# Layer 1 of a four-layer graph network: one joined float32r product for two weights of the turned h, and a new order of the steps around it

## The chip, the cores and the metric

The kernel runs on one core of a Trainium2 chip. The metric is the device time of one execution in microseconds, the median of several runs.

The engines are named as in the profile: PE multiplies matrices, PEld is its loading of the stationary operand, DVE, ACT and POOL work on elements, and SP issues the transfers (DMAs). Each engine takes its instructions in the order in which they were queued.

## What is computed

There are 32 graphs (batches) with the same 512 nodes and 128 features each, one 512x512 matrix `adj`, and four layers. Every layer is `x = x + layer(relu(layernorm(x)))`. Layer 1, the one that the change is in, is in the reference

```python
def _cheb_hops(x0, A, orders):
    x1 = jnp.einsum('bnf,nw->bwf', x0, A)
    ...
    x2 = 2.0 * jnp.einsum('bnf,nw->bwf', x1, A) - x0
...
xs = [X] + _cheb_hops(X, A1, 2) + _cheb_hops(X, A2, 2)
out = jax.nn.relu(stack(xs) @ Theta1 + bias)
```

with A1 and A2 both equal to `adj`. Since both hop lists are the same, the kernel adds up the five 128x128 blocks of Theta1 to three weights and computes, for h the normalised x,

- x1 = adj^T h,
- w = h th1 + x1 th2,
- x = x + relu(h th0 + adj^T w + b1).

Layer 0 is a masked attention with fixed scores, layer 2 a message layer with the squares of `adj` as its weights, and layer 3 an attention.

## The kernel before

**Names.** Two batches make a pair q (16 pairs). Two pairs make a round r of layer 1 (8 rounds), A = 2r and C = 2r + 1. Node blocks of 128 are counted by t or i (NT = 4). A product "of 512 columns" streams 512 columns of the moving operand past a 128x128 stationary one.

**Three parts.** Where a product must be nearly as exact as float32 but cheaper, both operands are split into three float32r tiles, `high`, `low` and `mid`, and the three products are added up in one PSUM bank. `moving_parts` (L420 to L422) makes them of an SBUF tile with one operation each on ACT, POOL and DVE; `bank_parts` does the like for a PSUM bank with one on ACT and two on DVE. The constants UP and DOWN belong to this splitting.

**The steps of layer 1**, all in `layer1` (L950 on):

- `normalised(q)`: h of a pair, eight ACT operations (L285), from statistics that DVE and ACT made before (`stats_steps`, L239 on).
- `turn(q)`: h is turned feature-major: DVE transposes 32x32 blocks, SP writes them to DRAM in four transfers (L328) and reads them back in one (L330). `straighten(q)` has POOL copy the result into `hs[q]` in plain order (L974).
- `split_up(q, b)`: the three parts of h of one batch.
- `first(q, b)`: x1 of one batch, turned, from the parts of h and of adj: twelve float32r products of 512 columns (L405), and one ACT copy out of PSUM (L407).
- `weighed(q, b)`: w of one batch: for each t two float32 products of 128 columns, `hs` with `th[:, 1]` and x1 with `th[:, 2]` (L447, through `projected`), and three operations that split the bank into the parts of w (L992 to L994).
- `mix(r, i)`: the output of one node block for the four batches of a round: four float32 products `hs` with `th[:, 0]` (L999), twelve float32r products of 512 columns, adj parts with w parts (L1003), then two DVE operations, one with the bias and one for relu and residual (L1005, L1007).

In the profile a float32 product is two instructions, a float32r product is one.

**What sets the order.** The kernel is laid out by hand: on PE, DVE, ACT and POOL the order of the calls in the source is the order of the queue. In round r the mixes of round r - 1 come first, then `first(A,1)`, the two `weighed` of A, the two `first` of C, the two `weighed` of C, and `first` of the next A. For layer 1's own turns the SP queue is ordered by the program builder; for the transfers of layer 2 and of the square it is the source order.

**Buffers.** `small_tile` has 13 buffers of 512 columns (parts of h, x1), `wide_tile` six of four times that (parts of w, the parts of the squared adj), the tag `hT` four (turned h before and after straightening), PSUM eight banks.

**What runs beside.** `square` (L1337 on) is a generator that loads `adj` in a crossed order, squares it and splits it into parts on POOL for layer 2; `go(square, n)` takes n steps of it. In the kernel before the load is in round 3 and the POOL steps lie in rounds 4 to 6. `ln_stats` makes the statistics of finished pairs for layer 2, one round after their mix. `more(step)` is the entry of layer 2: normalising, turning and fetching its first batches in the last round, and its first two `features`. `late_parts` makes the three weights `th` and the parts of adj, late in layer 0.

Of the kernel before, what the change touches and what calls it, by code (L numbers as in the profile page):

```python
# [9 lines left out]
F32 = mybir.dt.float32  # L10
# [19 lines left out]
def kernel(  # L30
# [369 lines left out]
    def mixed_parts(name, left, right, dst):  # L400

        p = bank(f"p_{name}")
        for part in range(3):
            for t in range(NT):
                nc.tensor.matmul(p, right[part][:, blk(t)], left[part][:, t, :],  # L405
                                 start=(t == 0 and part == 0), stop=(t == NT - 1 and part == 2))
        nc.scalar.activation(dst, p, AF.Copy, scale=UP)  # L407

    def three(name):
        return [small_tile(f"{part}_{name}", F32R) for part in PARTS]  # L410
# [7 lines left out]
    def moving_parts(x, high, low, mid):  # L418

        nc.scalar.activation(high, x, AF.Copy, scale=DOWN)  # L420
        nc.gpsimd.tensor_sub(low, x, high.bitcast(F32))  # L421
        nc.vector.scalar_tensor_tensor(mid, x, 1.0 / UP, high.bitcast(F32), OP.mult, OP.subtract)  # L422

    def scaled_parts(x_low, high, low, mid):

# [307 lines left out]
    def late_parts():  # L733

        adj_parts.extend(matrix_tile(f"adj_{part}", F32R) for part in PARTS[:2])
        high, low = adj_parts
        for t in range(NT):
            nc.scalar.activation(high[:, t, :], adj_s[:, t, :], AF.Copy, scale=DOWN)
            tc.keep_in_program_order(nc.gpsimd.tensor_sub(adj_s[:, t, :], adj_s[:, t, :], high[:, t, :].bitcast(F32)))
            yield  # L740
        for out, op, p, q in ((1, OP.add, 1, 3), (2, OP.add, 2, 4), (0, OP.subtract, 0, 2)):
            tc.keep_in_program_order(nc.gpsimd.tensor_tensor(th[:, out, :], th[:, p, :], th[:, q, :], op))
        tc.keep_in_program_order(nc.gpsimd.tensor_scalar(th[:, 2, :], th[:, 2, :], 2.0, None, OP.mult))
        nc.gpsimd.tensor_scalar(th[:, 0, :], th[:, 0, :], 1.0 / UP, None, OP.mult)
# [205 lines left out]
    def layer1(more, square):  # L950


        h, hT, hs, parts, x1, w = {}, {}, {}, {}, {}, {}
        normal, turning = {}, {}

        def normalised(q, n=2 * NT):
# [19 lines left out]
        def split_up(q, b):  # L976
            if q < NQ:
                parts[q, b] = three(f"h_{q}_{b}")
                moving_parts(h[q][:, b].rearrange("p t f -> p (t f)"), *parts[q, b])

        def first(q, b):
            if q < NQ:
                x1[q, b] = small_tile(f"x1T_{q}_{b}")
                mixed_parts(f"x1T_{q}_{b}", adj_parts, parts[q, b], x1[q, b])

        def weighed(q, b):
            r, j = q // 2, 2 * (q % 2) + b
            if j == 0:
                w[r] = [wide_tile(f"w_{part}_{r}", F32R) for part in PARTS]
            p = projected(f"p_w_{q}_{b}", (columns(hs[q][:, b]), th[:, 1, :]), (columns(x1[q, b]), th[:, 2, :]))  # L990
            high, low, mid = (part.rearrange("p t (w f) -> p t w f", f=D)[:, :, j, :] for part in w[r])
            nc.scalar.activation(high, p, AF.Copy, scale=DOWN)  # L992
            nc.vector.tensor_sub(low, p, high.bitcast(F32))
            nc.vector.scalar_tensor_tensor(mid, p, 1.0 / UP, high.bitcast(F32), OP.mult, OP.subtract)  # L994

        def mix(r, i):
            p = bank(f"p_l1_{r}_{i}")
            for j in range(4):
                nc.tensor.matmul(p[:, blk(j)], columns(hs[2 * r + j // 2][:, j % 2])(i), th[:, 0, :],  # L999
                                 start=(j == 0), stop=False, skip_group_check=True)  # L1000
            for part in range(3):
                for t in range(NT):
                    nc.tensor.matmul(p, adj_parts[part][:, t, blk(i)], w[r][part][:, t, :],  # L1003
                                     start=False, stop=(part == 2 and t == NT - 1), skip_group_check=True)
            nc.vector.scalar_tensor_tensor(tiles(p), tiles(p), UP, spread(b1, 4), OP.mult, OP.add)  # L1005
            x = xq[r].rearrange("p w b t f -> p (w b) t f")[:, :, i, :]
            nc.vector.scalar_tensor_tensor(x, tiles(p), 0.0, x, OP.max, OP.add)  # L1007

# [2 lines left out]
        turn(0)  # L1011
        normalised(1)
        yield
        split_up(0, 0)
        split_up(0, 1)
        first(0, 0)
        straighten(0)
        turn(1)
        for r in range(NQ // 2):
            A, C = 2 * r, 2 * r + 1  # L1020
            last = r == NQ // 2 - 1
            if r == 0:
                first(A, 1)
                split_up(C, 0)
                split_up(C, 1)
                straighten(C)
            else:
# [8 lines left out]
                mix(r - 1, 2)  # L1036
                split_up(C, 0)
                go(square, r > 3)
                mix(r - 1, 3)
                split_up(C, 1)  # L1040
                first(A, 1)
            weighed(A, 0)
            weighed(A, 1)
            if last:
                more(0)
            go(square, r > 2)
            first(C, 0)
            normalised(A + 2, NT)
            if last:
                more(1)  # L1050
            if r:
                ln_stats(A - 2)
            else:
                go(own[NQ - 3])
                go(own[NQ - 2])
            first(C, 1)
            if last:
                more(2)
            if r:
                straighten(C)  # L1060
            split_up(A + 2, 0)
            normalised(A + 2)
            go(square, r > 3)
            weighed(C, 0)
            weighed(C, 1)
            ln_stats(C - 2) if r else go(own[NQ - 1])
            go(square, r > 3)
            turn(A + 2)
            first(A + 2, 0)
            if r == 0:  # L1070
                normalised(C + 2, 0)
        more(3)
        for i in range(NT):
            mix(r, i)
# [179 lines left out]
    def layers_2_and_3():  # L1254
# [15 lines left out]
        for n in range(B):  # L1270
# [16 lines left out]
                fetch(2, 2)  # L1287
            elif n % 2 and n + 5 < B:
                fetch(2, n // 2 + 3)
            if n in (2, 3):  # L1290
                ln_stats(NQ - 4 + n)
            if n == 12:
                weights_of_3()
            if n == 20:
# [42 lines left out]
    def square():  # L1337

        raw = wide_tile("adj_crossed")
        load_crossed(raw, adj)  # L1340
        yield
        sq.extend(wide_tile(f"sq_{part}", F32R) for part in PARTS[:2])
        for i in range(NT):
            row, (high, low) = raw[:, i, :], (part[:, i, :] for part in sq)
            nc.gpsimd.tensor_mul(row, row, row)
            nc.gpsimd.tensor_scalar(split(high), crossed(row), DOWN, 1.0, OP.mult, OP.mult)
            yield
            nc.gpsimd.tensor_sub(crossed(row), crossed(row), split(high.bitcast(F32)))
            nc.gpsimd.tensor_scalar(split(low), crossed(row), LOW, 1.0, OP.mult, OP.mult)
            yield  # L1350
        sq.append(wide_tile(f"sq_{PARTS[2]}", F32R))
        for i in range(NT):
            high, low = (part[:, i, :].bitcast(F32) for part in sq[:2])
            nc.gpsimd.tensor_sub(sq[2][:, i, :], high, low)

    made_square = square()

    def more(step):

        if step == 0:  # L1360
            chunk(2, 0)
        elif step == 1:
            chunk(2, 1)
            turn_half(2, 0)
        elif step == 2:
            turn_half(2, 1)
        elif step == 3:
            fetch(2, 0)
            chunk(2, 2)
        elif step == 4:  # L1370
            turn_half(2, 2)
            chunk(2, 3)
        elif step == 5:
            turn_half(2, 3)
            features(0)
            chunk(2, 4)
        elif step == 6:
            fetch(2, 1)
# [51 lines left out]
```

## Time and profile before

| | us |
|---|---|
| median of 3 runs (912.77 to 913.18) | 912.8 |
| the profiled execution, its own time | 912.96 |
| its span, first to last instruction | 911.2 |
| PE busy in the span | 901.1 |
| layer 1's first product to layer 2's first message product, start to start | 183.6 to 450.6 |

The profile is one execution. A row of a timeline gives the start in us from the span's beginning, the length of the merged row in us, engine, line, operation, the tiles it writes and reads, the shape and the number of instructions. A row of a table of windows gives the stretch, its length, and for PE, PEld, DVE, ACT and POOL the busy us with the number of instructions, then the granted PE clock, the share of the DMA engines and GB/s. A row of waits gives who waited for whom, the us in total, how often, and the longest. Matmuls are pipelined: what one costs in a stream is read between starts, not from its own duration.

### The profile page before, as it was taken

The numbers are of one execution on the slowest core, as the hardware profiler recorded it, in microseconds if no ns is written. First come the engines' busy times: TensorE is split into PE (matmuls) and PEld (weight loads), VectorE is DVE, ScalarE is ACT, GpSimd is POOL, SyncE is SP. The second block draws the span as 40 slices with busy tenths as digits, with TensorE's granted clock in tenths as the row PEclk, the third lists the DMA queues.
The fourth block names the chain that finished last, engine by engine and source line by source line (L and its number), as shares of the span: only waits on it lengthen the run. The fifth ranks groups of instructions, "written<-read, shape, count | busy, mean of one in ns | idle before, by whom it ended". The sixth has DMA issues, their size and how long they took to land.

```text
span 911.2 us, 15170 instructions
## 1 busy us (share of the span) xinstructions
PE 901.1 (99%) x5432; PEld 774.2 (85%) x5433; DVE 669.7 (74%) x1348; ACT 527.5 (58%) x1156; POOL 485.6 (53%) x435
## 2 busy tenths in 40 slices
PE   8999999999999999999999999999999999999998
PEld 4899999988888888888877777777789999999998
DVE  7888886566656665665767777777698888987775
ACT  5874554343532442452556768876577767666663
POOL 5867999932132163342254445545475555666553
PEclk9999999999999999999999999999999999999999
DMA  9255644123114313212332344455212223222111
GB/s 265 50 167 165 186 122 118 24 71 93 35 59 119 87 31 90 71 46 76 106 120 70 93 126 129 132 147 160 70 48 82 81 82 91 73 70 81 59 36 47
DMA packets 83915, 86.06 MB, mean 94 GB/s; under 512 B 6784, under 2 KB 74624, under 8 KB 83840
## 3 DMA queue, kind: packets, MB, share of 16 engines
q1 hardware_dynamic: 83552, 84.57, 32.8%
q8 instruction: 43, 0.70, 0.3%
q10 hardware_dynamic: 288, 0.52, 0.2%
q14 instruction: 32, 0.26, 0.1%
HBM read 44.17 MB, written 40.89 MB: 93 GB/s over the span
## 4 chain that ended last, share of the span: by engine, by line
PE 92%; ACT 3%; DVE 3%; POOL 1%; issue 0%; DMA 0%; DVEq 0%; POOLq 0%; ACTq 0%
PE p_av L1234 12%; PE p_l L1003 10%; PE p_x1T L405 9%; PE p_score L1212 9%; PE p_msgT L1142 9%; PE p_w L447 6%; PE p_l_c L393 4%; PE p_l L999 3%; PE p_l_a L393 3%; PE p_l_d L393 3%; PE p_g L447 3%; PE p_l L447 3%; PE p_hv L447 3%; PE p_feat L447 3%; PE p_phi L1151 3%; PE p_phi L1152 3%
## 5 line engine op out<-in xcount | busy, mean ns | idle before, releaser
L1234 PEld LDWEIGHTS p_av<-hv,ex 128*128 128x128 f32 x1024 | 119.3, 191 | 3.7 <-POOL ex L1207 1.0
L1234 PE MATMUL p_av<-hv,ex 128*128 128x129 f32 x1024 | 119.8, 274 | 0.8 <-POOL ex L1207 0.8
L421 POOL TENSOR_TENSOR low_feat<-feat,high_feat 128x512 fp32r<-128x512 f32 x32 | 53.9, 1686 | 115.8 <-ACT high_feat L420 111.7
L285 ACT ACTIVATE h<-x,sh,rs 128x128 f32<-128x128 f32 x256 | 102.8, 483 | 11.8 <-DVE sh L257 11.0
L1207 DVE TENSOR_TENSOR ex<-ex,adjTx 128x512 f32<-128x512 f32 x64 | 80.4, 1259 | 35.7 <-ACT ex L1205 34.0
L1207 POOL TENSOR_TENSOR ex<-ex,adjTx 128x512 f32<-128x512 f32 x64 | 98.1, 1551 | 12.2 <-ACT ex L1205 8.1
L1093 ACT ACTIVATE h<-x,sh,rs 128x128 f32<-128x128 f32 x256 | 102.9, 485 | 0.0
L428 POOL TENSOR_TENSOR key<-key 128x512 fp32r<-128x512 f32 x32 | 50.2, 1567 | 97.9 <-DVE key L427 39.8
L421 POOL TENSOR_TENSOR low_h<-h,high_h 128x512 fp32r<-128x512 f32 x32 | 47.1, 1482 | 76.6 <-ACT high_h L420 76.4
L245 DVE BATCH_NORM_STATS2 bn<-x 128x6 f32<-128x256 f32 x244 | 85.9, 417 | 0.0
L407 ACT ACTIVATE x1T<-p_x1T 128x512 f32<-128x512 f32 x32 | 19.0, 594 | 109.4 <-PE p_x1T L405 100.8
L1205 ACT ACTIVATE ex<-ex 128x512 f32<-128x512 f32 x128 | 78.9, 651 | 0.0
L1213 ACT ACTIVATE ex<-p_score 128x512 f32<-128x512 f32 x128 | 74.0, 604 | 1.4 <-PE p_score L1212 1.1
L974 POOL COPY hs<-hT 128x512 f32<-128x512 f32 x32 | 18.6, 612 | 81.5 <-DMA hT<-d_hT 81.3
L432 ACT ACTIVATE high_query<-p_query 128x512 fp32r<-128x512 f32 x32 | 19.2, 599 | 73.8 <-PE p_query L1185 73.8
L422 DVE SCALAR_TENSOR_TENSOR mid_feat<-feat,high_feat 128x512 fp32r<-128x512 f32 x32 | 28.9, 904 | 44.3 <-ACT high_feat L420 44.3
L1212 PE MATMUL p_score<-high_query,key 128*128 128x512 f32 x128 | 50.5, 394 | 0.0
L1212 PE MATMUL p_score<-low_query,key 128*128 128x512 f32 x128 | 50.3, 393 | 0.0
L1212 PE MATMUL p_score<-mid_query,key 128*128 128x512 f32 x128 | 50.3, 393 | 0.0
L447 PE MATMUL p_w<-th,x1T 128*128 128x128 f32 x256 | 49.6, 275 | 0.3 <-ACT x1T L407 0.3
L254 ACT ACTIVATE sd<-bn,eps 128x8 f32<-128x8 f32 x46 | 13.9, 302 | 61.5 <-DVE bn L245 57.4
L447 PE MATMUL p_w<-th,hs 128*128 128x128 f32 x256 | 49.4, 275 | 0.0
(220 smaller groups left out, 2350.4 us busy)
## 6 DMA issues: line engine op xcount, KB each, us to landing
d<-hb SPq DMA_DIRECT2D x128, 128.0 KB, 2.5
hT<-d SPq DMA_DIRECT2D x32, 512.0 KB, 3.4
d_hT<-hb_hT SPq DMA_DIRECT2D x112, 128.0 KB, 2.4
hT<-d_hT SPq DMA_DIRECT2D x28, 512.0 KB, 3.3
x<-in_x_dram SPq DMA_DIRECT2D x32, 256.0 KB, 5.0
out_dram<-x SPq DMA_DIRECT2D x31, 256.0 KB, 2.3
adjT_d<-adj_squares SPq DMA_DIRECT2D x4, 256.0 KB
adj_crossed<-in_adj_dram SPq DMA_DIRECT2D x4, 256.0 KB
```

Of the source, the lines that this page charges most:

```text
L245: nc.vector.bn_stats(st[:, k].rearrange("p e s -> p (e s)"), xt[q][:, b, t : t + 2, :].rearrange("p t f -> p f t"))
L285: nc.scalar.activation(h[:, b, t, :], xt[q][:, b, t, :], AF.Relu, bias=shift[q][:, i : i + 1], scale=scale[q][:, i : i + 1])
L393: nc.tensor.matmul(p[:, i * 2 * D : (i + 1) * 2 * D], a[:, k, blk(i)], b[:, k], start=(first and i == 0 and k == 0), stop=(k == 1), skip_g ...
L405: nc.tensor.matmul(p, right[part][:, blk(t)], left[part][:, t, :], start=(t == 0 and part == 0), stop=(t == NT - 1 and part == 2))
L421: nc.gpsimd.tensor_sub(low, x, high.bitcast(F32))
L447: nc.tensor.matmul(p[:, blk(t)], hT(t), w, start=(i == 0), stop=(i == len(terms) - 1))
L1003: nc.tensor.matmul(p, adj_parts[part][:, t, blk(i)], w[r][part][:, t, :], start=False, stop=(part == 2 and t == NT - 1), skip_group_check= ...
L1093: nc.scalar.activation(h[:, t, :], xt[q][:, b, t, :], AF.Relu, bias=shift[q][:, i : i + 1], scale=scale[q][:, i : i + 1])
L1142: nc.tensor.matmul(p, feats[n][part][:, blk(t)], sq[part][:, t, :], start=(t == 0 and part == 0), stop=(t == NT - 1 and part == 2))
L1207: eng.tensor_mul(split(ex[:, t, :]), split(ex[:, t, :]), crossed(mask[:, t, :]))
L1212: nc.tensor.matmul(p, keys[n][i][:, t, :], query[n][i], start=(i == 0), stop=(i == 2))
L1234: nc.tensor.matmul(po[:, i, : D + 1], ex[:, t, blk(i0 + i)], hv[:, t, :], start=(t == 0), stop=(t == NT - 1))
```

## The change

1. `weighed`: the turned h is split into three parts as well (`split_turned`: ACT, POOL, DVE), and `th[:, 0:2]`, the weights of the own term and of w, are split once (`fixed_parts`). For each t, three float32r products of 256 columns give h th0 and h th1 side by side in one half of a PSUM bank; one float32 product of 128 columns adds x1 th2 to the second half. A batch takes two banks. Each bank is read by two ACT operations (the high part of w, and the own term, which goes back into `hs`) and two DVE operations (low and mid part of w), on 128x256 elements each.
2. The own term leaves `mix`: its four float32 products go, the bias is added to the own term by POOL (`biased_own`), and the first DVE operation of the mix adds the own term in place of the bias, in two halves.
3. `square`'s load is issued in four pieces in round 1, and its POOL work, now with a pause between the last four subtractions, lies in rounds 2 to 7, two steps in each.
4. The order within the rounds is new: A's second split before C's, C's straightening right behind `first(A,1)`, turns of the next A before the `weighed` of C, statistics one round later, so that those of two pairs more are made in layer 2.
5. The entry of layer 2 is moved ahead in the last round, between the mixes and the `weighed`.

```diff
+    def fixed_parts(x, high, low, mid):
+        nc.scalar.activation(high, x, AF.Copy, scale=DOWN)
+        nc.gpsimd.tensor_sub(x, x, high.bitcast(F32))
+        nc.scalar.activation(low, x, AF.Copy, scale=LOW)
+        nc.gpsimd.tensor_sub(mid, high.bitcast(F32), low.bitcast(F32))
...
-        nc.scalar.activation(dst, p, AF.Copy, scale=UP)
+        nc.scalar.copy(dst, p)
...
-        nc.gpsimd.tensor_scalar(th[:, 0, :], th[:, 0, :], 1.0 / UP, None, OP.mult)
...
+        def split_turned(q, b):
+            hs_parts[q, b] = three(f"hs_{q}_{b}")
+            moving_parts(hs[q][:, b], *hs_parts[q, b])
...
         def weighed(q, b):
...
-            p = projected(f"p_w_{q}_{b}", (columns(hs[q][:, b]), th[:, 1, :]), (columns(x1[q, b]), th[:, 2, :]))
-            high, low, mid = (part.rearrange("p t (w f) -> p t w f", f=D)[:, :, j, :] for part in w[r])
-            nc.scalar.activation(high, p, AF.Copy, scale=DOWN)
-            nc.vector.tensor_sub(low, p, high.bitcast(F32))
-            nc.vector.scalar_tensor_tensor(mid, p, 1.0 / UP, high.bitcast(F32), OP.mult, OP.subtract)
+            ps = [bank(f"p_w_{q}_{b}_{i}") for i in range(2)]
+            for t in range(NT):
+                p = ps[t // 2][:, t % 2 * 2 * D : (t % 2 + 1) * 2 * D]
+                for part in range(3):
+                    nc.tensor.matmul(p, hs_parts[q, b][part][:, blk(t)], th_parts[part],
+                                     start=(part == 0 and t % 2 == 0), stop=False, skip_group_check=True)
+                nc.tensor.matmul(p[:, D:], x1[q, b][:, blk(t)], th[:, 2, :], start=False, stop=True,
+                                 skip_group_check=True)
+            for i, p in enumerate(ps):
+                p = p.rearrange("p (t k f) -> p k t f", t=2, k=2)
+                high, low, mid = (part.rearrange("p t (w f) -> p t w f", f=D)[:, 2 * i : 2 * i + 2, j, :]
+                                  for part in w[r])
+                nc.scalar.activation(high, p[:, 1], AF.Copy, scale=UP * DOWN)
+                nc.scalar.activation(tiles(hs[q][:, b])[:, 2 * i : 2 * i + 2, :], p[:, 0], AF.Copy, scale=UP)
+                nc.vector.scalar_tensor_tensor(low, p[:, 1], UP, high.bitcast(F32), OP.mult, OP.subtract)
+                nc.vector.tensor_sub(mid, p[:, 1], high.bitcast(F32))
+
+        def biased_own(q):
+            for b in range(2):
+                nc.gpsimd.tensor_add(tiles(hs[q][:, b]), tiles(hs[q][:, b]), spread(b1, NT))
 
         def mix(r, i):
             p = bank(f"p_l1_{r}_{i}")
-            for j in range(4):
-                nc.tensor.matmul(p[:, blk(j)], columns(hs[2 * r + j // 2][:, j % 2])(i), th[:, 0, :],
-                                 start=(j == 0), stop=False, skip_group_check=True)
             for part in range(3):
...
-            nc.vector.scalar_tensor_tensor(tiles(p), tiles(p), UP, spread(b1, 4), OP.mult, OP.add)
+            for k in range(2):
+                pk = tiles(p)[:, 2 * k : 2 * k + 2, :]
+                nc.vector.scalar_tensor_tensor(pk, pk, UP, hs[2 * r + k][:, :, blk(i)], OP.mult, OP.add)
...
+        pair = small_tile("th_high", F32R), small_tile("th_low", F32R)
+        th_parts = pair[0][:, : 2 * D], pair[0][:, 2 * D :], pair[1][:, : 2 * D]
+        fixed_parts(th[:, 0:2, :].rearrange("p k f -> p (k f)"), *th_parts)
```

The order of a round from the second on, as it is after the change:

```python
split_up(A, 1)
straighten(A)
mix(r - 1, 0)
normalised(C, NT)
turn(C, 1)
mix(r - 1, 1)
go(early, NT)
normalised(C)
turn(C)
split_turned(A, 0)
mix(r - 1, 2)
split_turned(A, 1)
go(square, 2 if r > 1 else 1)
...
mix(r - 1, 3)
go(early)
first(A, 1)
split_up(C, 0)
straighten(C)
...
weighed(A, 0)
split_up(C, 1)
weighed(A, 1)
...
split_turned(C, 0)
first(C, 0)
go(late_stats, NT)
split_turned(C, 1)
turn(A + 2, 1)
first(C, 1)
go(late_stats, 1)
split_up(A + 2, 0)
turn(A + 2)
biased_own(A)
weighed(C, 0)
weighed(C, 1)
go(late_stats)
biased_own(C)
first(A + 2, 0)
```

Here `early` and `late_stats` are the statistics of pairs A - 4 and C - 4. Round 0 has its splits, turns and first three `first` ahead of the loop. In the last round `more(0)` stands ahead of the last mix, `more(1)` behind C's straightening and `more(2)` behind the `weighed` of A; `fetch(2, 0)` belongs to step 2 and `fetch(2, 1)` to step 5, one step earlier each, and the second `chunk` to step 0.

More of the change, by code (lines that the diff above doesn't have):

```diff
@@ L950, in layer1 @@
     def layer1(more, square):
-        h, hT, hs, parts, x1, w = {}, {}, {}, {}, {}, {}
+        h, hT, hs, parts, hs_parts, x1, w = {}, {}, {}, {}, {}, {}, {}
         normal, turning = {}, {}
@@ L1003, in mix @@
                     nc.tensor.matmul(p, adj_parts[part][:, t, blk(i)], w[r][part][:, t, :],
-                                     start=False, stop=(part == 2 and t == NT - 1), skip_group_check=True)
-            nc.vector.scalar_tensor_tensor(tiles(p), tiles(p), UP, spread(b1, 4), OP.mult, OP.add)
+                                     start=(part == 0 and t == 0), stop=(part == 2 and t == NT - 1))
+            for k in range(2):
+                pk = tiles(p)[:, 2 * k : 2 * k + 2, :]
+                nc.vector.scalar_tensor_tensor(pk, pk, UP, hs[2 * r + k][:, :, blk(i)], OP.mult, OP.add)
             x = xq[r].rearrange("p w b t f -> p (w b) t f")[:, :, i, :]
@@ L1013, in layer1 @@
         yield
+        pair = small_tile("th_high", F32R), small_tile("th_low", F32R)
+        th_parts = pair[0][:, : 2 * D], pair[0][:, 2 * D :], pair[1][:, : 2 * D]
+        fixed_parts(th[:, 0:2, :].rearrange("p k f -> p (k f)"), *th_parts)
         split_up(0, 0)
+        turn(1)
         split_up(0, 1)
+        normalised(2)
+        split_up(1, 0)
+        straighten(0)
         first(0, 0)
-        straighten(0)
-        turn(1)
+        split_turned(0, 0)
+        first(0, 1)
+        split_turned(0, 1)
+        first(1, 0)
+        straighten(1)
         for r in range(NQ // 2):
@@ L1021, in layer1 @@
             last = r == NQ // 2 - 1
[L1022 to L1027, printed above, removed]
+            early, late_stats = ((stats_steps(q) if r > 1 else iter(())) for q in (A - 4, C - 4))
+            if r:
                 split_up(A, 1)
@@ L1033, in layer1 @@
                 mix(r - 1, 1)
+                go(early, NT)
                 normalised(C)
                 turn(C)
+                split_turned(A, 0)
                 mix(r - 1, 2)
+                split_turned(A, 1)
+                go(square, 2 if r > 1 else 1)
+                go(early, 1)
+                normalised(A + 2)
+                if last:
+                    more(0)
+                mix(r - 1, 3)
+                go(early)
+                first(A, 1)
                 split_up(C, 0)
[L1038 to L1041, printed above, removed]
+                straighten(C)
+                if last:
+                    more(1)
+            go(square, r == 1)
             weighed(A, 0)
+            split_up(C, 1)
             weighed(A, 1)
             if last:
[L1045 to L1050, printed above, removed]
-            if r:
[L1052 to L1060, printed above, removed]
+                more(2)
+            split_turned(C, 0)
+            first(C, 0 if r else 1)
+            go(square, r == 1)
+            go(late_stats, NT)
+            split_turned(C, 1)
+            turn(A + 2, 1)
+            if r:
+                first(C, 1)
+            go(late_stats, 1)
             split_up(A + 2, 0)
-            normalised(A + 2)
-            go(square, r > 3)
+            turn(A + 2)
+            biased_own(A)
             weighed(C, 0)
             weighed(C, 1)
-            ln_stats(C - 2) if r else go(own[NQ - 1])
-            go(square, r > 3)
-            turn(A + 2)
+            go(late_stats)
+            biased_own(C)
+            go(square, r == 1)
             first(A + 2, 0)
@@ L1071, in layer1 @@
                 normalised(C + 2, 0)
+                for q in (NQ - 3, NQ - 2, NQ - 1):
+                    go(own[q])
         more(3)
@@ L1289, in layers_2_and_3 @@
                 fetch(2, n // 2 + 3)
-            if n in (2, 3):
-                ln_stats(NQ - 4 + n)
+            if n in (2, 3, 4, 5):
+                ln_stats(NQ - 6 + n)
             if n == 12:
@@ L1339, in square @@
         raw = wide_tile("adj_crossed")
-        load_crossed(raw, adj)
-        yield
+        rows_of = adj.rearrange("(a b c) w -> b a c w", a=NT, c=QR)
+        for b in range(NQR):
+            tc.keep_in_program_order(nc.sync.dma_start(raw[:, b, :], rows_of[b]))
+            yield
         sq.extend(wide_tile(f"sq_{part}", F32R) for part in PARTS[:2])
@@ L1354, in square @@
             nc.gpsimd.tensor_sub(sq[2][:, i, :], high, low)
+            yield
     made_square = square()
@@ L1361, in more @@
             chunk(2, 0)
+            chunk(2, 1)
         elif step == 1:
-            chunk(2, 1)
             turn_half(2, 0)
@@ L1366, in more @@
             turn_half(2, 1)
+            fetch(2, 0)
         elif step == 3:
-            fetch(2, 0)
             chunk(2, 2)
@@ L1374, in more @@
             turn_half(2, 3)
+            fetch(2, 1)
             features(0)
@@ L1377, in more @@
         elif step == 6:
-            fetch(2, 1)
             features(1)
```

## The prediction

> **What bounds the kernel now.** I read the page's busy shares first, then the table of windows, the waits of the matmul engine (PE), and the order of its instructions in one round of layer 1.
>
> ```profile
> PE 901.1 (99%) x5432; PEld 774.2 (85%) x5433; DVE 669.7 (74%) x1348; ACT 527.5 (58%) x1156; POOL 485.6 (53%) x435
> ...
> PEclk9999999999999999999999999999999999999999
> ```
>
> ```profile
> 387.00:420.00 33.00, 33.00 (x193) 28.72 (x192) 19.99 (x38) 13.29 (x30) 13.14 (x13) 1.00 0.24 65
> ```
>
> The second block is one round of layer 1: length, then PE, weight loads, DVE, ACT and POOL. PE is busy for 33.00 of 33.00 us at the full clock; DVE is busy 20.0, ACT 13.3, POOL 13.1. Over the whole layer PE's only recorded wait is this:
>
> ```profile
> PE p_w L447 <- ACT x1T L407: 0.3, 1, 0.3
> ```
>
> So layer 1 is as long as PE's instruction list. What one instruction costs has to be read from start to start, because the durations of pipelined matmuls overlap:
>
> ```profile
> 394.53 1.08 PE L405 MATMUL p_x1T<-adj_high,high_h 128*128 128x512 f32 x4
> 395.45 1.09 PE L405 MATMUL p_x1T<-adj_low,low_h 128*128 128x512 f32 x4
> 396.38 1.10 PE L405 MATMUL p_x1T<-adj_mid,mid_h 128*128 128x512 f32 x4
> 397.31 0.38 PE L447 MATMUL p_w<-th,hs 128*128 128x128 f32 x2
> 397.53 0.39 PE L447 MATMUL p_w<-th,x1T 128*128 128x128 f32 x2
> 397.76 0.39 PE L447 MATMUL p_w<-th,hs 128*128 128x128 f32 x2
> ...
> 403.66 1.05 PE L999 MATMUL p_l<-th,hs 128*128 128x128 f32 x8
> 404.47 1.19 PE L1003 MATMUL p_l<-w_high,adj_high 128*128 128x512 f32 x4
> 405.49 1.09 PE L1003 MATMUL p_l<-w_low,adj_low 128*128 128x512 f32 x4
> 406.42 1.09 PE L1003 MATMUL p_l<-w_mid,adj_mid 128*128 128x512 f32 x4
> ```
>
> A full-precision product of 128 columns is recorded as two instructions and takes 0.223 us (397.31 to 397.53 to 397.76). A float32r product of 512 columns is one instruction of 0.231 us (four in 0.92). A batch therefore costs 12 x 0.231 = 2.78 (first), 8 x 0.223 = 1.79 (weighed), and, as a quarter of four mixes, 4 x 0.223 = 0.89 and 2.78: 8.24, or 33.0 for the four of a round, which is the window's length.
>
> **PE's part of the change.** Gone per batch: 12 full-precision products, 12 x 0.223 = 2.68 us (eight in weighed, four own terms in the mix). Come: 12 float32r products of 256 columns, and four full-precision ones stay (x1 with weight 2), 0.89. What a float32r product of 256 columns costs, c, no row shows. Near rows are 0.231 at 512 columns and, in layer 0, a full-precision stream at 256:
>
> ```profile
> 180.17 1.89 PE L393 MATMUL p_l_d<-g,sums_att 128*128 128x256 f32 x8
> 181.69 1.08 PEld L791 LDWEIGHTS p_l_d<-w,hd 128*128 128x128 f32 x8
> 181.90 1.05 PE L791 MATMUL p_l_d<-w,hd 128*128 128x128 f32 x8
> ```
>
> That is 1.73 / 8 = 0.216 per instruction. The weight loads are no hindrance: each 128-column instruction has its own and still comes every 0.112. If float32r scales with its columns, c = 0.231 / 2 = 0.116. If what it has above the bare column rate is fixed, c = 0.231 - 0.216 / 2 = 0.123 (0.108 being half the 256-column row, the time that 256 columns take once). The Trainium skill (TensorE: Matmul & The Clock Gate, Back-to-back issue gap) gives columns / 2.4 + 2.5 ns at full clock: 0.109 here. By that rule 512 columns cost 0.216, and the trace has 0.231, so it is a floor: it would save 32 x (2.68 - 0.89 - 12 x 0.109) = 15.3 us; 0.123 saves 9.9. I take 0.118, between the two row values and the rule: 32 x (1.79 - 1.42) = 11.8 us. Switching between the two kinds costs nothing visible (L999's eight starts plus 8 x 0.112 lead to 404.55, and the low group starts 0.93 later, at 405.49), so I charge nothing for the eight switches per batch; the outer bound of c is 0.216, as if float32r gave nothing at this width.
>
> **The other engines, per round.** New work, by nearest row: ACT four high parts of turned h at 0.62 (L420) and sixteen half-bank reads at 0.37 (the layer-0 ACT copies of 128x256, L342) in place of four whole ones at 0.59: +2.5 +3.5, so 13.3 becomes 19.3. DVE four mid parts (L422, 0.69 alone), eight half-bank splits more (sixteen at 0.42, L357's row, for eight at 0.69) and the mix's bias step in two halves (eight at 0.42 for four at 0.70): +2.8 +1.2 +0.6, so 20.0 becomes 24.6. POOL four low parts at 1.3 to 1.8 (L421) and four bias adds at 1.28 (as L841): +11, plus two square steps, 3.8; 8.2 without square becomes 23. PE's new round is 33.0 - 4 x 0.37 = 31.5. None reaches it on busy time. Statistics run a round later, and those of two pairs move into layer 2, 1.8 us of DVE and 0.3 of ACT each; in the first 185 us of layer 2 PE is busy for 183.6 and DVE for 136.5, so they hide there too. The one POOL step removed (a 128x128 scaling, once) was hidden before.
>
> The rule that speaks against the change is the skill's note (Advanced Engine Details and Errata, VectorE Performance Modes, Mode Summary) that VectorE's second port is shared with GpSimd, so that two-port operations and GpSimd work block each other. The trace agrees:
>
> ```profile
> 398.71 1.77 POOL L421 TENSOR_TENSOR low_h<-h,high_h 128x512 fp32r<-128x512 f32 x1 [3.47 <-ACT high_h L420]
> 405.99 1.29 POOL L421 TENSOR_TENSOR low_h<-h,high_h 128x512 fp32r<-128x512 f32 x1 [5.50 <-ACT high_h L420]
> ```
>
> The first runs beside DVE's mid_h; elsewhere DVE's grows from 0.69 to as much as 1.76. By that rule all eight mids (1.3 each) and all POOL subtractions (1.8) of a round are slow: DVE 24.6 + 8 x 0.6 = 29.4, POOL 27. Still under 31.5, so it takes reserve, not time; if DVE passed 31.5 each further us of it would cost eight over the layer.
>
> **Waits that the change adds.** What matters is latency on in-order queues. I follow a round from its first mix with PE at 2.78 a mix or first and 2.31 a weighed: mixes to 11.1, first(A,1) 13.9, weighed(A) 18.5, first(C) 24.1, weighed(C) 28.7, first(A+2,0) 31.5.
> - The small buffers are 13; two now hold the weights' parts, so splits wait for PE to finish a reader: C's first split for first(A,1) at 13.9 (needed from 18.5), its second for weighed(A,0) at 16.2 (needed at 21.3), the turned C split for weighed(A,1). ACT stands in these waits with the half-bank evictions behind it, which nobody needs sooner.
> - Turned C is the tight one. It goes through DRAM:
>
> ```profile
> 406.63 7.00 SPq L328 DMA_DIRECT2D d_hT<-hb_hT  x5
> 413.80 0.34 SPq L330 DMA_DIRECT2D hT<-d_hT  x1
> 414.18 1.44 SPq L328 DMA_DIRECT2D d_hT<-hb_hT  x3
> 419.20 0.34 SPq L330 DMA_DIRECT2D hT<-d_hT  x1
> ```
>
> Its last transpose ends at 413.3 and POOL's straightening starts at 423.6: 10.3 us. In the new order the transpose ends near 9.3 (mix 1 out at 7.1, statistics 1.4, transpose 0.7), so straightening runs 19.6 to 20.8. Behind it on POOL stand the low part of h(C,1), to 22.1, wanted at 22.2, and that of turned (C,0), to 23.6, wanted at 24.2. Before, straightening was needed only as an unsplit stationary. Reserve about 0.1 to 0.6 us, against rows of 1.29 to 1.77.
> - biased_own(C) stands on POOL for the evictions of weighed(C,1); behind it is only the next round's low part, wanted 10 us later, and DVE's mix step, wanted at 34.
> - The w parts of (C,1) are ready some 1.5 us after weighed(C,1); first(A+2,0) covers 2.8. Without that cover the mix would wait the 1.5.
> - Start of layer 1: four operations on 128x256 go ahead of the first split. POOL is at adj_mid until 180.3; then about 0.7 + 0.4 + 0.6 + 0.7 put its low part at 183.3, used at 184.6. Hidden, by 1.3; if not, up to 1.5, once.
> - Square: its row loads sit singly on SP's queue in round 1, its POOL steps, 3.8 a round, ahead of low(C,0). POOL is idle then, as low(C,0) waits for first(A,1). If that cover is gone, 3.8 in a round, less the reserve.
> - Layer-2 entry: features(2) needs its transposed h some 9.6 us after mix 1; PE gets there after 10.1 (12 before). Nothing, or 1 to 2 once.
> None of these can gain more than PE's old 0.3. The zero end is no wait at all; the far end is 1.4 a round (a late low part behind another slow one), 11 in all. I take 0.2 in each of seven rounds and 0.2 for start and entry: 1.6, near the zero end, because each item has some cover of its own.
>
> **Sum.** On the profiled execution: span 911.2 - 11.8 + 1.6 = 901.0; with the 1.76 around it (912.96 - 911.2) 902.8. The median of the runs, 912.8, is 0.2 below that execution: 902.6.
>
> **Rivals.** (1) The turned-h chain sets the round. Against: it has its cover on paper. For: three POOL steps in line with at most 0.6 in hand. At 0.6 to 1.4 a round over seven or eight rounds, 4 to 11 us: 907 to 912, hardly any gain. (2) float32r is no faster than full precision at 256 columns: c = 0.216, 12 x 0.216 + 0.89 = 3.48 against 2.68, +0.80 x 32 = +25.7: 938.5, slower. It decides from c = 1.79 / 12 = 0.149. For: every float32r row has 512 columns; against: a single instruction there takes 0.231 where the full-precision one takes two. (3) The edit works better than I charge: c at the floor and no waits, 897.5.
>
> **How the numbers follow.** Forecast with (3), waits up to 3 us and c from 0.109 to 0.123: 0.76, times 897.5 to 906. Rival 1: 0.15, of which 0.10 faster, 0.04 the same, 0.01 slower. Rival 2: 0.09. That is 0.86 faster, 0.04 same, 0.10 slower; 0.2% (1.8 us) is about what a measurement of this kernel can tell from no change. The range 897 to 909.5 takes the forecast and near half of rival 1, about 0.82.
>
> **What would show it.** Right: float32r rows on p_w 0.11 to 0.125 apart; a round of 31 to 32 us with PE full; DVE 24 to 29 in it. Wrong: starts 0.2 apart (rival 2); PE waiting on DVE or POOL for the turned parts ahead of weighed(C,0) or first(C,1) (rival 1); DVE without gaps.

## The result and the profile after

The changed kernel takes 905.4 us (median of 4 runs, 905.06 to 906.11) against 912.8: the ratio is 0.9919, with an interval of 0.9902 to 0.9936. It is 7.4 us faster; 10.2 were forecast. The profiled execution took 905.41 us, its span is 903.6.

Where the time went is seen best by stages, each from the start of one PE group to the next: layer 1 from the first product of x1 to the first message product, layer 2 from there to the first attended product of layer 3.

| us | before | after | difference |
|---|---|---|---|
| layer 0, to layer 1's first product | 183.6 | 183.7 | +0.1 |
| layer 1 | 267.0 | 256.9 | -10.1 |
| one round of it (first mix to first mix, the middle ones) | 33.05 | 31.57 | -1.5 |
| layer 2 | 211.5 | 214.0 | +2.5 |
| the rest of the span | 249.1 | 249.1 | 0.0 |

Layer 1 gave what the shorter list promises, less something at its start; layer 2, which the change hardly touches, gave 2.5 back.

The busy shares after the change, and one round from first mix to first mix, before and after (length, then PE, weight loads, DVE, ACT, POOL, and the granted PE clock):

```profile
PE 891.2 (99%) x5304; PEld 761.8 (84%) x5305; DVE 707.0 (78%) x1476; ACT 569.5 (63%) x1286; POOL 579.7 (64%) x500
```

```profile
371.40:404.47 33.07, 33.07 (x196) 28.77 (x194) 20.03 (x37) 13.29 (x30) 13.25 (x12) 1.00 0.24 64
366.90:398.54 31.64, 31.64 (x178) 27.28 (x176) 25.93 (x52) 18.37 (x46) 22.04 (x19) 1.00 0.24 67
```

PE is still busy for the whole of the round. DVE has 25.9 us (24.6 were worked out), ACT 18.4 (19.3), POOL 22.0 (23). In a round PE's rows of weighed look like this; each row is one instruction, or the two of a float32 product:

```profile
223.49 0.36 PE L1006 MATMUL p_w<-th_high,high_hs 128*128 128x256 f32 x1
223.69 0.28 PE L1006 MATMUL p_w<-th_high,low_hs 128*128 128x256 f32 x1
223.81 0.28 PE L1006 MATMUL p_w<-th_low,mid_hs 128*128 128x256 f32 x1
223.93 0.38 PE L1008 MATMUL p_w<-th,x1T 128*128 128x128 f32 x2
...
225.79 0.36 PE L1006 MATMUL p_w<-th_high,high_hs 128*128 128x256 f32 x1
```

The float32r products of 256 columns start 0.12 apart. Four blocks (one batch) take 225.79 - 223.49 = 2.30 us, so the three float32r products and the float32 one of a block take 0.575, and the cost of one float32r product of 256 columns, the prediction's c, is (0.575 - 0.223) / 3 = 0.117. The loss at the start of layer 1 is in PE's waits (us in total, times, longest):

```profile
PE p_w L1006 <- POOL low_hs L421: 1.1, 2, 0.9
PE p_w L1006 <- DVE mid_hs L422: 0.2, 1, 0.2
```

Both lie in round 0. On POOL and PE, in order of time:

```profile
188.32 1.80 POOL L421 TENSOR_TENSOR low_h<-h,high_h 128x512 fp32r<-128x512 f32 x1 [1.86 <-ACT high_h L420]
190.06 1.17 POOL L980 COPY hs<-hT 128x512 f32<-128x512 f32 x2
191.42 3.47 POOL L421 TENSOR_TENSOR low_hs<-hs,high_hs 128x512 fp32r<-128x512 f32 x2 [0.19 <-ACT high_hs L420]
```

```profile
192.13 0.28 PE L1006 MATMUL p_w<-th_high,high_hs 128*128 128x256 f32 x1
193.26 0.38 PE L1006 MATMUL p_w<-th_high,low_hs 128*128 128x256 f32 x1 [0.85 <-POOL low_hs L421]
```

The straightening of pair 0 stands on POOL behind the low part of batch (1,0), which waits for ACT: the eight normalisations of pair 2 come first there. So the low part of turned (0,0) is ready at 193.2, and PE, which reached it at 192.2, waits.

In layer 2 a message step takes PE 6.29 us; the steps are counted from 0. Some of the first sixteen are longer: before the change five, by 2.4 us together, after it six, by 4.95. The longest after it is step 7 with 8.91 (PE's message products start at 481.94 and again at 490.85). In that step PE waits twice:

```profile
487.38 1.12 PE L1192 MATMUL p_phi<-msgT,phi 128*128 128x512 f32 x2 [0.67 <-DVE msgT L1319]
489.93 1.16 PE L454 MATMUL p_l<-phi,msgT 128*128 128x128 f32 x8 [1.43 <-ACT msgT L1193]
```

The first wait is for DVE's scaling of the message (L1319). DVE comes to it late, because the statistics of two pairs stand in front of it:

```profile
481.09 0.68 DVE L1201 TENSOR_TENSOR x<-p_l,x 128x512 f32<-128x512 f32 x1
481.69 1.43 DVE L245 BATCH_NORM_STATS2 bn<-x 128x6 f32<-128x256 f32 x4
483.50 0.20 DVE L256 RECIPROCAL rs<-sd 128x8 f32<-128x8 f32 x1 [0.37 <-ACT sd L252]
483.74 0.17 DVE L257 SCALAR_TENSOR_TENSOR sh<-bn,rs 128x8 f32<-128x8 f32 x1
483.82 1.43 DVE L245 BATCH_NORM_STATS2 bn<-x 128x6 f32<-128x256 f32 x4
485.62 0.20 DVE L256 RECIPROCAL rs<-sd 128x8 f32<-128x8 f32 x1 [0.37 <-ACT sd L254]
485.86 0.17 DVE L257 SCALAR_TENSOR_TENSOR sh<-bn,rs 128x8 f32<-128x8 f32 x1
486.04 0.71 DVE L1142 STREAM_TRANSPOSE hb<-h 128x512 f32<-128x512 f32 x1
486.67 0.65 DVE L1319 TENSOR_SCALAR msgT<-p_msgT 128x512 f32<-128x512 f32 x1
```

One set belongs to an updated pair, the other to pair 15. The kernel before makes the sets of pairs 14 and 15 at message steps 2 and 3; with pairs 12 and 13 moved in ahead of them, they come at steps 4 and 5. Each set is four sums (1.43 us), a wait of 0.37 for ACT's square root and two small steps.

### The profile page after: what moved, and what is told of

Read it like the earlier page. It is cut to its first block, busy times and chain, and to the rows that moved or that the text cites. A ratio compares the mean times of both kernels' runs of the same rounds, so it can differ in the third digit from the quotient of the medians.

```text
span 903.6 us, 15432 instructions
## 1 busy us (share of the span) xinstructions
PE 891.2 (99%) x5304; PEld 761.8 (84%) x5305; DVE 707.0 (78%) x1476; ACT 569.5 (63%) x1286; POOL 579.7 (64%) x500
## 4 chain that ended last, share of the span: by engine, by line
PE 84%; DVE 5%; ACT 4%; POOL 3%; issue 2%; DMA 1%; SPq 1%; DVEq 0%; POOLq 0%; ACTq 0%
PE p_av L1274 12%; PE p_l L1027 9%; PE p_score L1252 9%; PE p_x1T L405 9%; PE p_msgT L1182 6%; PE p_w L1006 5%; PE p_l_c L393 4%; PE p_l_a L393 3%; PE p_l_d L393 3%; PE p_g L454 3%; PE p_hv L454 3%; PE p_w L1008 3%; PE p_l L454 2%; PE p_query L1225 2%; PE p_phi L1191 2%; PE p_phi L1192 2%
## 5 line engine op out<-in xcount | busy, mean ns | idle before, releaser
L421 POOL TENSOR_TENSOR low_h<-h,high_h 128x512 fp32r<-128x512 f32 x32 | 54.6, 1705 | 47.7 <-PE p_w L1008 28.6
L422 DVE SCALAR_TENSOR_TENSOR mid_feat<-feat,high_feat 128x512 fp32r<-128x512 f32 x32 | 25.5, 798 | 44.3 <-ACT high_feat L420 44.3
L421 POOL TENSOR_TENSOR low_hs<-hs,high_hs 128x512 fp32r<-128x512 f32 x32 | 44.4, 1399 | 14.2 <-ACT high_hs L420 13.8
L407 ACT COPY x1T<-p_x1T 128x512 f32<-128x512 f32 x32 | 18.8, 586 | 52.2 <-PE p_x1T L405 52.2
L454 PEld LDWEIGHTS p_l<-phi,msgT 128*128 128x128 f32 x256 | 33.0, 191 | 18.3 <-issue 10.5
```

The lines of the kernel that those rows point to most:

```text
L454: nc.tensor.matmul(p[:, blk(t)], hT(t), w, start=(i == 0), stop=(i == len(terms) - 1))
```

## The experiments

Each kernel is the changed one with the edit shown, unless it is said otherwise. The times are medians; "layer 1" and "layer 2" are the stages of the table above, from each one's profiled execution. The kernel before took 912.6 to 913.2 beside them.

| kernel | us | ratio to before, interval | layer 1 | layer 2 |
|---|---|---|---|---|
| the change | 905.4 | 0.9919 (0.9902 to 0.9936) | 256.9 | 214.0 |
| statistics at even steps | 905.8 | 0.9925 (0.9912 to 0.9937) | 256.9 | 214.2 |
| before, with the later statistics | 915.4 | 1.0026 (1.0015 to 1.0036) | 266.9 | 212.9 |
| pair 0 straightened first | 904.4 | 0.9906 (0.9892 to 0.9919) | 255.8 | 213.5 |
| not joined | 943.8 | 1.0337 (1.0323 to 1.0351) | 296.5 | 212.1 |
| two statistics back in layer 1 | 903.0 | 0.9898 (0.9883 to 0.9913) | 258.0 | 210.6 |
| both of these | 902.1 | 0.9885 (0.9872 to 0.9899) | 256.9 | 210.7 |
| order alone | 916.3 | 1.0040 (1.0027 to 1.0052) | 267.5 | 214.1 |
| longer straightening | 907.4 | 0.9944 (0.9930 to 0.9957) | 259.5 | 213.4 |
| both, another place | 903.3 | 0.9894 (0.9879 to 0.9909) | 258.0 | 210.8 |
| bare sums | 902.9 | 0.9890 (0.9873 to 0.9906) | 258.1 | 210.4 |
| roots on POOL | 903.5 | 0.9893 (0.9878 to 0.9908) | 256.9 | 211.6 |
| roots on POOL, pair 0 first | 902.5 | 0.9882 (0.9865 to 0.9898) | 255.8 | 211.7 |

In two rows, statistics at even steps and order alone, layer 2 of the profiled execution holds about 1.6 us that come from a lower PE clock; this is shown at order alone.

**Statistics at even steps.** The first theory of layer 2's loss was that two sets in one message step are too many.

```diff
-            if n in (2, 3, 4, 5):
-                ln_stats(NQ - 6 + n)
+            if n in (2, 4, 6, 8):
+                ln_stats(NQ - 5 + n // 2)
```

> The changed kernel with the statistics of the last four pairs made at message steps 2, 4, 6 and 8 of layer 2 instead of 2, 3, 4 and 5, so that none falls into an odd step, where the statistics of an updated pair are made too. Theory (two statistics in one step put 3.6 us of DVE in front of the message's scaling, and PE stalls for it; that is the 2.5 us that layer 2 became longer): step 7's 8.9 us falls to about 6.3 to 6.6, layer 2 loses 2 to 2.5 us, 902.9 to 903.4. Rival (layer 2 is longer because its entry got less time ahead of it, and the lag of DVE comes from there): the stall only moves, 905 to 905.6.

Step 7 did fall to 6.29, but steps 9 and 10 rose to 7.33 and 8.76 with new waits, the longest 1.47 for ACT, and the kernel is no faster. That theory fell: the wait moves with the statistics. Step 11 rose to 7.54 without a wait: from 509.7 to 513.1 PE's granted clock was 0.50 in this execution.

**Before, with the later statistics.** The kernel before, with this edit alone (and the same for pair C):

```diff
-            if r:
-                ln_stats(A - 2)
-            else:
+            if r > 1:
+                ln_stats(A - 4)
+            elif r == 0:
...
-            if n in (2, 3):
-                ln_stats(NQ - 4 + n)
+            if n in (2, 3, 4, 5):
+                ln_stats(NQ - 6 + n)
```

> The kernel before, with nothing of the change but its statistics: one round later in layer 1, and those of four pairs at message steps 2 to 5 of layer 2. Theory (the doubled statistics cost layer 2 its 2.5 us): layer 1 as before, layer 2 longer by 1 to 2.5 us, 914 to 915.3. Rival (the shorter entry costs it): 912.6 to 913.1.

Its step 7 takes 8.92 us, as in the changed kernel, with the old entry into layer 2. So the moved statistics make this wait, and the shorter entry does not. By the medians the kernel is 2.6 us slower than before, but in its profile layer 2 is only 1.4 longer. That execution is one of three (914.3) with a mean granted clock of 1.000 of full speed; the other five, with 0.998, took 915.3 to 916.2. So 1.4 us are the waits; the rest came only with the lower clock, and no profile of such an execution of this kernel was kept.

**Pair 0 straightened first.**

```diff
         split_up(0, 1)
+        straighten(0)
         normalised(2)
         split_up(1, 0)
-        straighten(0)
```

> The changed kernel with pair 0 straightened on POOL before the split of batch (1,0) instead of after it, at the start of layer 1. Theory (PE's wait of about 1.1 us for the low part of turned h ahead of the first weighed comes from POOL standing in the later split, which waits for eight normalisations on ACT): the wait goes, 904.2 to 904.6. Rival (ACT's high part is late anyway, or the wait returns at the next weighed): 905.0 to 905.6.

Layer 1 became 1.1 us shorter and the kernel 1.0: the start's wait was POOL's order.

**Not joined.** The same work with two products of 128 columns for each one of 256:

```diff
-                    nc.tensor.matmul(p, hs_parts[q, b][part][:, blk(t)], th_parts[part],
-                                     start=(part == 0 and t % 2 == 0), ...
+                    for k in range(2):
+                        nc.tensor.matmul(p[:, blk(k)], hs_parts[q, b][part][:, blk(t)], th_parts[part][:, blk(k)],
+                                         start=(part == 0 and t % 2 == 0 and k == 0), ...
```

> The changed kernel with each float32r product of 256 columns done as two of 128 columns with the same stationary part. It tells what the joining is worth. If a float32r product of 128 columns costs what its weight load allows, about 0.11, weighed goes from 2.30 to 8 x 3 x 0.11 + 0.89 = 3.5 us and the kernel to 905.4 + 32 x 1.2 = 945. If the cost is by columns (0.06), nothing changes: 905 to 907. If float32r loses its speed below 256 columns (0.22, as a float32 product of 128), weighed is 6.2 us and the kernel near 1030.

Here are PE's rows of one block, two instructions each, and one of the next block:

```profile
264.82 0.39 PE L1007 MATMUL p_w<-th_high,low_hs 128*128 128x128 f32 x2
265.05 0.39 PE L1007 MATMUL p_w<-th_low,mid_hs 128*128 128x128 f32 x2
...
265.71 0.39 PE L1007 MATMUL p_w<-th_high,low_hs 128*128 128x128 f32 x2
```

From 264.82 to 265.71, a block of six such products and the float32 one takes 0.89 us, so (0.89 - 0.223) / 6 = 0.111 for a float32r product of 128 columns, against 0.117 for 256. Half the columns cost nearly the same. That points to the weight load which each instruction brings: by the Trainium skill (TensorE: Matmul & The Clock Gate, LDWEIGHTS) a load takes columns of the stationary part / 1.2, by estimate 107 ns for 128, a little under the measured spacing. The trace records each load as 0.19 us long, with one load overlapping the next, so it does not show that figure by itself, and no run here varied the load alone. Without the joining the change would be 31 us slower than before.

**Two statistics back in layer 1.** Those of pairs 12 and 13, in its last round:

```diff
                 go(early)
+                if last:
+                    ln_stats(A - 2)
                 first(A, 1)
...
             biased_own(A)
+            if last:
+                ln_stats(C - 2)
             weighed(C, 0)
...
-            if n in (2, 3, 4, 5):
-                ln_stats(NQ - 6 + n)
+            if n in (2, 3):
+                ln_stats(NQ - 4 + n)
```

> The changed kernel with the statistics of pairs 12 and 13 made in the last round of layer 1, where DVE is busy for 26 of 31.6 us a round, instead of in layer 2; those of 14 and 15 stay at message steps 2 and 3, as in the kernel before. Theory (in layer 2 DVE with its waits for ACT has next to no room, so each of the two extra statistics there comes out as PE wait, wherever it is put): the first stall falls away or shrinks, layer 2 is 2 to 2.5 us shorter, 902.9 to 903.5. Rival (the shorter entry leaves DVE late, whoever made the statistics): 905 to 905.6.

Layer 2 fell by 3.4 us to 210.6, below the kernel before; layer 1's last round became 1.1 longer (first mix to first mix 28.7 to 29.8), which leaves 2.4.

**Both of these.** The two edits together.

> The last experiment together with pair 0 straightened first at the start of layer 1, which alone gave 904.4. Theory: both add up, 901.8 to 902.4. Rival: layer 1 starts layer 2 a microsecond sooner and the wait comes back there, 902.9 to 904.4.

902.1 us: they add up. This is the fastest of all the kernels here.

**Order alone.** The joined product is undone: weighed and mix as before, no split of turned h, no bias step on POOL.

> The changed kernel without the joined product: weighed, the own term in the mix, the bias step and the products are those of the kernel before, there is no split of the turned h and no bias step on POOL; only the new order, the spread square, the later statistics and the earlier entry stay. Theory (all the gain is PE's shorter list, and the order by itself only costs what the two extra statistics cost in layer 2): layer 1 as before within 0.5 us, layer 2 up to 2.5 longer, 913.5 to 915.5. Rival (the order gains by itself): below 912.

916.3, some 0.8 above the upper end of what was expected. Two of its five executions, with a mean granted clock of 1.000 and 0.999, took 915.4; three, with 0.998 or 0.997, took 916.3 to 917.9. The profiled one is the longest of them, and its windows around the end of step 7 show where the clock goes (the granted clock stands behind POOL's count):

```profile
497.04:501.70 4.66, 2.54 (x9) 0.88 (x8) 3.14 (x6) 3.74 (x9) 0.94 (x1) 1.00 0.01 2
501.70:505.10 3.40, 3.40 (x13) 2.92 (x13) 3.27 (x5) 2.74 (x8) 2.16 (x3) 0.50 0.12 27
```

PE waits 0.69 and 1.43 us in step 7, as in the changed kernel; then its clock is 0.50 for 3.4 us. The products from 501.31 to 505.75 take 4.44 us, where the same ones take 2.84 in the changed kernel, whose clock stayed at 1.00. So 1.6 of the 2.6 us that layer 2 is longer come from the clock, and 1.0 from waits. Layer 1 is 0.5 longer, for a wait of 0.6 at its start, and layer 0 1.3, of which 1.1 is one wait for a DMA. What makes the executions at 915.4 longer beyond 0.5 and 1.0 is open.

The new order gains nothing by itself; all the gain comes with the shorter list of products. Whether the shorter list would have gained as much in the old order was not tried.

**Longer straightening.** From pair 3 on, each pair C is copied three times over:

```diff
-            for b in range(2):
+            for b in (0, 1) * (3 if q % 2 and q > 1 else 1):
```

> The changed kernel with POOL's two straightening copies of each pair C from round 1 on done three times over (same data, same result): 2.4 us more on POOL ahead of the low parts of h(C,1) and of turned (C,0). It measures the reserve of the turned-h chain. By the reserve of the prediction, 0.1 to 0.6 us, each of seven rounds loses 1.8 to 2.3 us: 918 to 921.5. By the trace of the changed kernel, where the low part of h(C,1) ends at 386.9 and is wanted at 389.3, the reserve is 2.3: 905.4 to 906.5.

The reserve by the trace of the changed kernel is read from these two rows, the low part of h(C,1) on POOL and its first use by PE:

```profile
385.17 1.75 POOL L421 TENSOR_TENSOR low_h<-h,high_h 128x512 fp32r<-128x512 f32 x1
389.25 1.09 PE L405 MATMUL p_x1T<-adj_low,low_h 128*128 128x512 f32 x4
```

907.4 us lies between the two forecasts. Five of the seven rounds hold their length within 0.15 us, two lose 1.3 and 0.9, in all 2.6. So the turned-h chain had about 2.3 us in hand in most rounds, and 1.1 and 1.5 in two: in the first, whose writes to DRAM begin 11.1 us after its first mix instead of 9.4, and in the fourth, whose read is issued 5.3 us after the first write instead of 3.7. The prediction's 0.1 to 0.6 was too small: in these two rounds POOL starts on the turned h 7.4 and 8.8 us after the first write, not 10.3.

**Both, another place.** As "both of these", with the statistics of pair 13 between `turn(A + 2, 1)` and `first(C, 1)`.

> Pair 0 straightened first and the statistics of pairs 12 and 13 in the last round of layer 1, as in the version that gave 902.1, but those of pair 13 ahead of first(C,1), where the last round has no turn of a next pair, instead of ahead of weighed(C,0). There the last round had become 1.1 us longer, with PE waiting 0.6 for the high part of w. Theory (DVE's order in the last round alone made that): last round 28.7 to 28.9, 900.8 to 901.4. Rival (the statistics cost the round 1.1 wherever they stand): 902.

Neither came: 903.3, and the last round became longer still, 30.9 us. ACT's rows there (in brackets, how long it stood idle before and for whom) show why:

```profile
425.35 0.30 ACT L254 ACTIVATE sd<-bn,eps 128x8 f32<-128x8 f32 x1 [5.11 <-DVE bn L245]
425.56 0.56 ACT L407 COPY x1T<-p_x1T 128x512 f32<-128x512 f32 x1
```

ACT's square root waits for DVE's sums, and behind it in ACT's queue stands the copy of x1 that PE needs; PE waits 1.7 us for that copy. A set of statistics is small, but ACT stands at its root until DVE has come to the sums in its own queue.

**Bare sums.** The version with two statistics back in layer 1, and in message steps 4 and 5 DVE's sums of two pairs once more, unused. The edit takes pairs 14 and 15, not 12 and 13 as the expectation says; the work is the same:

```diff
+            if n in (4, 5):
+                st = stats.tile([P, NT, 2, 3], F32, tag="bn", name=f"bn_more_{n}", bufs=4)
+                for k in range(NT):
+                    b, t = divmod(2 * k, NT)
+                    nc.vector.bn_stats(...)
```

> The version with the statistics of pairs 12 and 13 in layer 1 (903.0), with the four DVE sums of each of them done once more at message steps 4 and 5 of layer 2, their result unused and without the square root on ACT and the two small DVE steps behind it. Theory A (DVE's own time is what layer 2 lacks: 2 x 1.43 us): layer 2 is 1.5 to 2.5 us longer, 904.5 to 905.5. Theory B (it is DVE and ACT waiting for each other at the square root, not DVE's time): 902.9 to 903.4.

902.9, as without them: 2.9 us more of DVE cost nothing in sum. Steps 7 and 9 are 0.3 longer each, and a wait of 1.0 at step 15 is gone in return. The full sets of the changed kernel make steps 6, 7, 9 and 11 longer by 3.9 in all against this version without the sums.

**Roots on POOL.** The changed kernel, with everything behind the sums of the last four pairs done by POOL:

```diff
+        nc.gpsimd.tensor_scalar(sd, st[:, :, :, 2], 1.0 / D, EPS, OP.mult, OP.add)
+        nc.gpsimd.tensor_scalar(sh, st[:, :, :, 1], -1.0, None, OP.mult)
+        nc.gpsimd.tensor_tensor(rs, sd, minus_half, OP.pow)
+        nc.gpsimd.tensor_mul(sh, sh, rs)
...
-                ln_stats(NQ - 6 + n)
+                pool_stats(NQ - 6 + n)
```

> The changed kernel, statistics of the last four pairs at message steps 2 to 5 of layer 2 as in it, but behind DVE's four sums everything is done by POOL (the root as a power), so that neither ACT's square root nor DVE's two small steps that wait for it stand in the queues. Theory (what those statistics cost layer 2 is DVE and ACT waiting for each other, since DVE's bare sums cost nothing): layer 2 falls from 214.0 to about 210.5, 902 to 902.8. Rival (any statistics of those pairs there cost, by what they keep waiting behind them): 904.5 to 905.5.

> The same with pair 0 straightened first at the start of layer 1, which alone took 1.0 us off. If both hold they add up, and the last round of layer 1 stays at 28.7 us: 901 to 901.8, below the 902.1 of the version with the statistics moved into layer 1. If the wait comes back in layer 2: 902 to 904.5.

Layer 2 fell by 2.4 us to 211.6, not by the 3.4 that it gave to take two of the four sets out; the kernels took 903.5 and 902.5, 0.7 us above what was expected of each. Most of the cost goes with the root's way over ACT and back; 1.0 us stays, now at steps 9 and 11, where PE waits for ACT.

## Why the prediction was right, and where it was not

**PE's list.** c was taken at 0.118 and is 0.117. The list is 32 x (2.68 - 2.30) = 12.2 us shorter; 11.8 were predicted. Between the two rows (0.116 by columns, 0.123 with a fixed part) the one by columns is nearer; at 128 columns a product still takes 0.111, so cost by columns holds at the width that the change uses and no longer at half of it. What switching between the kinds of product costs is inside c: a block has two switches, and with c at 0.1155 they would be 0.006 us together, so next to nothing, as assumed. Rival 2, no speed at this width, did not come. Its size was wrong: 0.216 is one instruction of 256 columns, and a full-precision product has two, 0.432, so "no faster than full precision" would have made the kernel slower by 32 x (12 x 0.432 + 0.89 - 2.68) = 109 us, not by 25.7.

**The engines.** Busy times were within 1.3 us of the sum on each, and none became the bound in layer 1. Operations that slow each other are there, and in the steady rounds they cost reserve only. The prediction reads its two rows of POOL as one beside DVE's mid part and one alone; in the trace both have company. At 398.71 POOL's subtraction took 1.77 and the mid part, begun at 398.66, 0.69; at 405.99 the subtraction took 1.29 and the mid part, begun at 406.52, 1.30. In these two pairs the one that began second was the longer one, so 29.4 for DVE and 27 for POOL, with all of both slow, counted too much (25.9 and 22.0 were measured).

**The turned-h chain.** 0.2 us were charged in each of seven rounds; the rounds show no such wait of PE, and the reserve is about 2.3 in most of them, not 0.1 to 0.6. The step that failed is the 10.3 us taken from the old trace. There the turns of A and C came within 8 us of each other, and A's read from DRAM (413.80) lay among C's writes; in the new order the turns are 14 to 18 us apart, and mostly the read is issued 3.7 to 3.9 us after the first write.

**The start of layer 1.** It was charged at next to nothing, "up to 1.5, once" if not hidden. From the first product to the first adj product of a mix it took 22.5 us before and 25.3 after, 2.84 more, of which the lists account for 4 x (2.30 - 1.79) - 0.89 = 1.15; so it lost 1.7, but not at the weights' split that the prediction named: PE has no wait for it. Most of it was the straightening of pair 0 behind a split that waits for ACT; the queue behind each POOL step was followed for the steady round and not for the start. Putting one line earlier took 1.1 of it away; of the other 0.6, two shorter waits for parts of the turned h, 0.16 and 0.23, still stand in that kernel's profile.

**Layer 2.** Here a step of the prediction is wrong: the statistics of two pairs "hide there too", argued from DVE busy for 136.5 of 185 us. That share is an average and says nothing of what stands in front of what. Moved there alone, into the kernel before, they make layer 2 1.4 us longer at the full clock (the median, with lower clocks, is 2.6 higher), and moved back out of the changed kernel they give 3.4 in layer 2. Busy time is not what is short: the bare sums made new waits of 0.6 us where the full sets made 3.9, and nothing in sum. What the full statistics have beside the sums is the root on ACT, for which DVE waits 0.37 and behind which ACT's own queue stands until DVE has come to the sums; with it on POOL most of the cost is gone. Whether it is DVE's 0.75 us per set behind the sums (the wait and two small steps) or ACT's queue held by the root that PE feels in layer 2 was not separated; in the last round of layer 1 the second is seen directly. What the remaining 1.0 us is stays open too. Of the 2.5 that layer 2 became longer, 0.6 belongs to the entry, as far as the profile tells: step 2 went from 6.61 to 7.18, and PE waits there 0.33 for the DMA that brings its turned h. That is within what the prediction allowed for it.

**Sum.** 12.2 - 1.7 (start) - 0.4 (what is left in layer 1, not followed one by one) - 2.5 (layer 2) = 7.6, against the 7.55 between the spans. The forecast had 11.8 - 1.6 = 10.2; the term mis-sized is the waits, 4.6 instead of 1.6, and the largest part of it, about 1.9 (2.5 - 0.6), is one that had been put at zero. PE's list was right for the reason given. The waits were not: most of them stand in places that the prediction did not name, and the total came near because the list is the larger term.

## What to carry to other kernels

A product is priced from start to start in a stream, and two products that share a stationary operand can be worth joining where they are narrow: here two of 128 columns cost 0.222 us and one of 256 cost 0.117. When small steps are moved to a stage "with room", do not read the room from busy shares: a step that goes from one in-order engine to another and back holds both queues, so look which work that the busiest engine waits for stands behind it. And a new order needs following at its start and end as carefully as in its steady state.

## What the runs showed that was not expected

A float32r product with its own weight load costs 0.111 us at 128 columns, 0.117 at 256 and 0.231 at 512: going from 256 columns to 128 saves 5%. Waits in layer 2 are not additive: 2.9 us more of DVE made two steps 0.3 longer and removed a wait of 1.0 that stood at step 15 otherwise. Perhaps an early wait of PE lets the engines behind it catch up; that was not tried by itself.

A wait of PE can cost more than its length. In the two profiled executions with the lower clock, 3.4 us at 0.50 began about half a microsecond after PE had taken up work again: in order alone PE had stood 2.1 of the 3.4 us before, with 1.43 as the longest single wait, in statistics at even steps 1.6 with 1.47. The changed kernel stood for the same 2.1 us and kept 1.00 in its profile, so the waits do not bring it every time; what decides it no run here shows.
